# A four-layer megakernel on one core: the prologue and two seams listed in another order, a lead of 80 scores, and the last two token blocks finished one after the other

## The chip, the core and the metric

The kernel runs on one core of a Trainium2 chip. The metric is device time in microseconds (us) for one execution of the whole program. TensorE (PE in the profile, with PEld for its weight loads), VectorE (DVE), ScalarE (ACT), GpSimd (POOL) and SyncE (SP, which issues nearly all DMAs) each run their own queue in order. They wait for each other through semaphores.

## What is computed

The input is `x` of 2 x 2048 x 256 in float32. Four residual layers follow each other, each on a layer norm of `x`:

```python
x = x + attn_a(layernorm(x))     # softmax attention, 16 heads, 4 kv heads, head size 16
x = x + ffn(layernorm(x))
x = x + attn_b(layernorm(x))     # causal linear attention: (q k^T * tril) v, rope, gate, norm
x = x + ffn(layernorm(x))        # the same weights as the first ffn

def ffn(x):
    gf = global_net(x.mean(axis=1))            # 256 -> 128 -> 64 -> 1, gelu, sigmoid
    out = x
    for _ in range(3):
        tf = coupling_net(out)                 # 256 -> 256 -> 128 -> 64 -> 1, gelu, sigmoid
        coupling = 0.1 + adaptive_range * (0.7 * gf + 0.3 * tf - 0.5) * 2
        out = out + coupling * twist(out)      # twist swaps and negates quarters of the features
    return out
```

## The kernel before

The 4096 tokens are eight blocks of 512 (`BLK`), four to each of the two batches. The program is one straight list of instructions. `in_order` (L136 onwards) ties each engine to the order in which the Python code emitted its instructions, so the order of the calls in the source is the order in every queue.

**First attention.** A unit is one block of queries and one of four groups of heads, 32 units in all. `largest()` (L361 to L420) is a generator. Each `next(ahead)` emits one score matmul `s` (L376) into one of three PSUM banks and one VectorE maximum `mx` (L380) over it; there are 64 of them to a unit. After a unit's 64 comes the reduction `nm` (L390) and its split into two parts `mt` (ACT L397, POOL L398). The turn of the maxima `mr` (DVE L403) follows behind the fourth score of the next unit, as `turning.pop()()`, and then eight small DMAs (L407, L412) carry the result to `a_m`. The main loop (from L636) takes a unit in 16 steps `kb`. Each step emits four `next(ahead)`, four score matmuls `p` (L648) with the maximum added by another matmul (L652), four exponentials on ScalarE (L656) and eight passes of `av` (L633) for the step before.

**Prologue.** Before that loop, blocks of `x` arrive and are normalised, turned into feature planes (`features`, L131 and L302), and projected to keys (`keys`, `pk` L309), values (`pv` L326) and queries (`asked`, `pq` L336). `look(j)` (L270 to L276) takes a block's statistics on VectorE and GpSimd. `spread(j)` (L290) normalises it on ScalarE. Keys go through memory and back by DMA (`stored` L246, `fetch` L251). `rows()` is a generator of three pieces. The first issues nine DMAs on SP (L216, eight for the output weights `a_wo`; L217, the bias `a_bo`). The second multiplies the identity by the bias on GpSimd (`a_db`, L221). The third spreads it over the partitions by a matmul (`a_pb`, L226) and copies it out on VectorE (`a_bo_row`, L227); the row is first used by the addition at L467, when the first unit is finished. `pieces()` yields 22 times: six queries of blocks 1 to 3, then for each of the blocks 4 to 7 features, keys, and the two halves of the queries (with the values). The loop over `LEAD` interleaves them with the scores:

```python
LEAD, MORE, WARM = 64 + 10, 6, 6
for n in range(4, LEAD):
    next(ahead)
    if (n % 3 == 1 and n < 55) or (n > 63 and n % 2 == 0):
        next(rest, None)
```

So 17 pieces stand three scores apart, eleven scores then stand alone, and five pieces follow two scores apart. Six scores more (`MORE`) are emitted in odd steps `kb` of unit 0, after which the maxima are 80 ahead.

**The rest.** `behind()` holds the other three layers. `ps` is a ring of seven PSUM banks, and `ps_state` holds one more bank for the running state `b_sums` of the linear attention. In the feed-forward layers, blocks go in pairs `k` (0 to 11: three cycles of four pairs). `first` (L817) and `second` (L827) are the first two matmul layers, `third` (L839) is the third, with both blocks of a pair in one bank and one gelu, and `fourth` is the last layer, the coupling and the addition. In cycles one and two `fourth` works on feature planes with VectorE and GpSimd (L857 to L864). In the last cycle (`back`, L886 onwards) it gives one coupling per token (L891, L896 to L898), turns the planes back (`turn_back`, L875, L879) and adds the twist on VectorE (L912), and in the last layer it stores the block (L918). `context` (L777 onwards) is the global net, a generator: the first `next` reduces the sums on VectorE (`gmf`, L781, L782), the second runs the first matmul (`p1f`, L786).

Two seams are listed by hand. Between the first feed-forward layer and the linear attention, the last pair's `fourth(11)` stands among the queries and keys of block 0 (`zero.query()`, `zero.rotate()`, `zero.key()`). Between the linear attention and the last layer, `x.next_turn()`, `third(1)`, `context` of batch 1, `fourth(1)` and `second(2)` follow each other. The program ends with `second(11)`, in which the two blocks are turned back early (`turn_ahead`), `third(11)` and `fourth(11)`.

Of the kernel before, what the change touches and what calls it, by code (L numbers as in the profile page):

```python
# [11 lines left out]
AF = mybir.ActivationFunctionType  # L12
# [4 lines left out]
P = 128  # L17
# [50 lines left out]
def tile_hybrid(ctx: ExitStack, tc: tile.TileContext, x: bass.AP, consts: bass.AP, wa_d: bass.AP, wf_d: bass.AP, wb_d: bass.AP, out: bass.AP):  # L68
# [28 lines left out]
    def tokens(j):  # L97
        return xs[:, 4 * j : 4 * j + 4, :]
# [54 lines left out]
    def attention_a():  # L153
        with ExitStack() as st:
# [206 lines left out]
            def largest():  # L361


                turning = []
                for u, (j, g) in enumerate(units):
                    k0 = (j // BPB) * N
                    qP = queries[u]
                    mx = sb.tile([P, KV, 4, 4], F32, tag="mx", name=f"mx{u}")
                    first = u == 0

                    def step(kb, qi, r):

# [3 lines left out]
                        mm(  # L376
                            s, qP[r // 2][row, qi * P : (qi + 1) * P],
                            kP[r // 2][row, k0 + kb * BLK : k0 + (kb + 1) * BLK], start=True, stop=True,
                        )
                        nc.vector.tensor_reduce(mx[:, r, qi : qi + 1, kb], s, AX.X, ALU.max)  # L380

                    for kb in range(4):
                        for qi in range(4):
                            for r in (0, 1, 3, 2):
                                step(kb, qi, r)
                                if (kb, qi, r) == (0, 0, 2) and turning:
                                    turning.pop()()
                                yield
                    nm = sb.tile([P, KV, 4], F32, tag="nm", name=f"nm{u}")
                    nc.vector.tensor_reduce(nm, mx, AX.X, ALU.max, negate=True)  # L390

                    mt = sb.tile([P, KV, 2, 4], F32, tag="mt", name=f"mt{u}")
# [24 lines left out]
                    if first or u + 1 == len(units):  # L417
                        turn_maxima()
                    else:
                        turning.append(turn_maxima)  # L420
# [83 lines left out]
                        nc.vector.tensor_tensor(pair, pair, po.rearrange("p (t d) -> p t d", t=2), ALU.add)  # L504
                        yield


            LEAD, MORE, WARM = 64 + 10, 6, 6
            ahead = largest()
            begin = len(nc.cur_bb.bb.instructions)  # L510
            loads = ExitStack()
# [81 lines left out]
            def pieces():  # L593

                memsets()
                look(4)
                values(3)
                for j in range(1, BPB):
                    for m in range(2):
                        asked(j, m)  # L600
                        yield
                        if (j, m) == (2, 0):
                            spread(4, ld, 0)
                next(more)
                for j in range(BPB, NB):
                    features(j, ld, 0)
                    if j + 1 < NB:
                        look(j + 1)
                    yield
                    keys(j, ld)()  # L610
                    if j + 1 < NB:
                        spread(j + 1, ld, 0)
                    yield
                    asked(j, 0)
                    yield
                    asked(j, 1)
# [21 lines left out]
            for u, kb in ((u, kb) for u in range(len(units)) for kb in range(KB)):  # L638
# [85 lines left out]
    def behind(tail):  # L724
# [18 lines left out]
        def bank(name):  # L743
            return ps.tile([P, BLK], F32, tag="ps", name=name)
# [28 lines left out]
        def rotations(n, part, store):  # L773
# [70 lines left out]
            def fourth(k, between=None):  # L844
# [8 lines left out]
                for e in range(2):  # L853
# [9 lines left out]
                    nc.vector.tensor_tensor(z[:, 0, :], z[:, 0, :], t0, ALU.add)  # L863
                    nc.gpsimd.tensor_tensor(z[:, 1, :], z[:, 1, :], t1, ALU.subtract)  # L864

            def turn_back(k, e, h):

                j = blocks(k)[e]
# [9 lines left out]
                for s in range(2):  # L878
                    nc.vector.tensor_tensor(half[:, :, s, :], half[:, :, s, :], tr[:, :, 1 - s, :], ALU.add)  # L879
                return half, tr  # L880

            def turn_ahead(k, e):
                for h in range(2):
# [2 lines left out]
            def back(k, js, a3, between):  # L886
# [12 lines left out]
                for e in range(2):  # L899
                    j = js[e]  # L900
                    if e == 1 and between:
                        between()
                    for h in range(2):
                        half, tr = turned.pop((k, e, h), None) or turn_back(k, e, h)
                        for q in range(2):
                            tile = 2 * h + q

                            x4, t4 = (
                                a.rearrange("p s (u f) -> p (s u) f", u=2) for a in (half[:, q, :, :], tr[:, q, :, :])
                            )  # L910
                            for m, quarters in enumerate((slice(0, 4, 3), slice(1, 3))):
                                nc.vector.scalar_tensor_tensor(  # L912
                                    x4[:, quarters, :], t4[:, quarters, :], cs[:, m, 2 * tile + e : 2 * tile + e + 1],
                                    x4[:, quarters, :], ALU.mult, ALU.add,
                                )
                        if store:
                            s0 = (j % BPB) * BLK + 2 * h * P
                            nc.sync.dma_start(  # L918
                                out[j // BPB, s0 : s0 + 2 * P, :].rearrange("(t p) d -> p t d", p=P),
                                tokens(j)[:, 2 * h : 2 * h + 2, :],  # L920
                            )

            return context, first, second, third, fourth, turn_ahead


        sums1 = hold.tile([P, 2, NB], F32, name="sums1")
# [280 lines left out]

        def rounds(f, n):

            context, first, second, third, fourth, _ = f  # L1210
            k = n // 2
            if n % 2 == 0:
                if 0 <= k - 2:
# [9 lines left out]
                    first(k, 1)  # L1223

        f = rotations(0, sums0, False)
        context, first, second, third, fourth, _ = f
        turned, looked = first_norms, {}

        def block_of(j):
# [92 lines left out]
        one.turn()  # L1322

        f = rotations(1, sums1, True)
        context, first, second, third, fourth, turn_ahead = f
# [211 lines left out]
```

## Time and profile before

| | |
|---|---|
| three timed runs | 2127.65, 2130.35, 2135.94 us; median 2130.35 us |
| the profiled execution | 2133.95 us, of which the span from the first to the last instruction is 2132.2 us |
| mean granted TensorE clock | 0.990 |
| PE busy | 2101.0 us (99%) |
| DVE busy | 1700.7 us (80%) |
| ACT busy | 1427.6 us (67%) |
| POOL busy | 355.6 us (17%) |

The span splits by stage, at the first exponential of unit 0 and the last one of unit 31: the prologue is the first 107.8 us, the softmax attention runs to about 1528 us, the first feed-forward layer to about 1710 us, the linear attention to about 1976 us, and the last layer to the end. Busy time counts matmuls that are waiting inside a pipeline, and their ends are modelled, so 99% doesn't say that TensorE is at its peak. The granted clock is the share of full speed that the hardware let TensorE run at. In a timeline, a row has the start, the length, the engine, the line and operation, the tiles, the count, and in brackets the idle time of that engine before it and what ended it.

### The profile page before, as it was taken

Reading aid. Unit: us, or ns where it says so; the run is one execution under the profiler, and the core shown is the slowest. Engines: PE = TensorE matmul, PEld = TensorE weight load, DVE = VectorE, ACT = ScalarE, POOL = GpSimd, SP = SyncE. Lnnn points to the kernel's source line nnn. Section 1 sums busy time; section 2 is a strip of 40 time slices with the busy share of each in tenths; the row PEclk is TensorE's granted clock in tenths of the full one; section 3 lists DMA queues with packets and bytes.
Section 4 is the critical chain, followed back from the end, with each engine's and each line's share of the span. In section 5 each row is a group of like instructions: output and inputs, shape, how many; then the busy total and the mean of one; then the engine's idle time right before and its main releaser. Section 6 shows DMA issues by size and latency. Waiting matters only on the chain.

```text
span 2132.2 us, 38745 instructions
## 1 busy us (share of the span) xinstructions
PE 2101.0 (99%) x14158; PEld 1018.7 (48%) x14158; DVE 1700.7 (80%) x3241; ACT 1427.6 (67%) x2787; POOL 355.6 (17%) x352
## 2 busy tenths in 40 slices
PE   9899999999999999999999999999999999999998
PEld 4344444444444444444444444444443567776434
DVE  7689998998999999899899899987134688886335
ACT  4377777777777877777777777777864445554443
POOL 3100000001001000000000000000135355551450
PEclk9799999999999999999999999999999999999999
DMA  6320110101101011010110101100100000000002
GB/s 204 92 88 10 49 37 17 47 10 47 37 19 37 18 49 39 18 38 20 47 37 20 37 19 48 38 18 8 52 1 1 0 2 1 2 1 2 0 0 79
DMA packets 59695, 68.71 MB, mean 32 GB/s; under 512 B 24944, under 2 KB 34032, under 8 KB 59248
## 3 DMA queue, kind: packets, MB, share of 16 engines
q1 hardware_dynamic: 58592, 64.79, 11.2%
q8 instruction: 111, 1.82, 0.4%
q10 hardware_dynamic: 720, 0.92, 0.1%
q14 instruction: 80, 0.66, 0.1%
q0 software_dynamic: 192, 0.52, 0.1%
HBM read 35.78 MB, written 26.21 MB: 29 GB/s over the span
## 4 chain that ended last, share of the span: by engine, by line
PE 93%; DVE 3%; issue 1%; ACT 1%; POOL 1%; DMA 1%; SPq 0%; DVEq 0%; POOLq 0%; ACTq 0%
PE av L633 24%; PE s L376 22%; PE p L648 11%; PE q1f L817 8%; PE p L652 7%; PE q2f L827 4%; PE pe L1117 2%; PE bpo L1143 2%; PE po L499 1%; PE pq L975 1%; PE pk L975 1%; PE pw L984 1%; PE pv L984 1%; DVE mx L380 1%; PE q3f L839 1%
## 5 line engine op out<-in xcount | busy, mean ns | idle before, releaser
L380 DVE TENSOR_REDUCE mx<-s 128x1 f32<-128x512 f32 x2048 | 1272.7, 683 | 110.7 <-PE s L376 106.4
L656 ACT ACTIVATE e<-p 128x512 f32<-128x512 f32 x2048 | 1057.7, 603 | 312.8 <-PE p L652 305.9
L376 PE MATMUL s<-a_kP,qP 64*128 64x512 f32 x2048 | 707.0, 471 | 4.8 <-DVE mx L380 2.8
L652 PE MATMUL p<-a_m,a_pick 64*128 64x512 f32 x2048 | 586.5, 415 | 0.0
L376 PEld LDWEIGHTS s<-a_kP,qP 64*128 64x128 f32 x2048 | 283.5, 184 | 567.4 <-DVE mx L380 550.8
L633 PE MATMUL av<-e,a_v 128*32 128x512 f32 x4096 | 546.8, 605 | 0.0
L648 PE MATMUL p<-qP,a_kP 64*128 64x512 f32 x2048 | 527.5, 394 | 2.5 <-ACT e L656 2.5
L648 PEld LDWEIGHTS p<-qP,a_kP 64*128 64x128 f32 x2048 | 286.9, 185 | 64.6 <-ACT e L656 25.5
L652 PEld LDWEIGHTS p<-a_m,a_pick 64*128 64x128 f32 x2048 | 284.6, 184 | 26.1
L817 PE MATMUL q1f<-zq,wf 128*128 128x512 f32 x384 | 175.7, 600 | 0.0
L633 PEld LDWEIGHTS av<-e,a_v 128*32 128x32 f32 x4096 | 81.0, 108 | 129.2 <-issue 121.2
L818 ACT ACTIVATE a1f<-q1f,wf 128x512 f32<-128x512 f32 x96 | 65.8, 686 | 102.2 <-PE q1f L817 99.0
L398 POOL TENSOR_TENSOR mt<-nm,mt 128x16 f32<-128x16 f32 x31 | 6.9, 221 | 736.3 <-ACT mt L397 736.3
L817 PEld LDWEIGHTS q1f<-zq,wf 128*128 128x128 f32 x384 | 70.5, 190 | 97.4 <-issue 84.9
L827 PE MATMUL q2f<-a1f,wf 128*128 128x512 f32 x192 | 90.7, 616 | 0.0
L1123 DVE TENSOR_TENSOR en<-pe,small 128x512 f32<-128x512 f32 x128 | 79.4, 683 | 11.3 <-PE pe L1117 11.2
L237 POOL TENSOR_TENSOR ql<-zq,qh 128x512 f32<-128x512 f32 x15 | 19.3, 1286 | 359.5 <-ACT qh L234 359.5
L858 DVE TENSOR_SCALAR cf<-cf,f_beta,alphaf 128x512 f32<-128x512 f32 x32 | 33.6, 1050 | 54.0 <-ACT cf L857 54.0
L862 POOL TENSOR_TENSOR tf<-cf,zq 128x512 f32<-128x512 f32 x32 | 56.6, 1768 | 93.5 <-DVE cf L858 93.1
L829 ACT ACTIVATE a2f<-q2f,wf 128x512 f32<-128x512 f32 x48 | 32.6, 685 | 53.3 <-PE q2f L827 53.3
L827 PEld LDWEIGHTS q2f<-a1f,wf 128*128 128x128 f32 x192 | 35.6, 195 | 45.8 <-issue 44.7
L864 POOL TENSOR_TENSOR zq<-zq,tf 128x512 f32<-128x512 f32 x32 | 56.8, 1776 | 2.5
(209 smaller groups left out, 1633.5 us busy)
## 6 DMA issues: line engine op xcount, KB each, us to landing
qP<-dq SPq DMA_DIRECT2D x64, 256.0 KB
dq<-qh SPq DMA_DIRECT2D x62, 128.0 KB
dq<-ql SPq DMA_DIRECT2D x62, 128.0 KB
a_kP<-dk SPq DMA_DIRECT2D x16, 256.0 KB
oc<-avs SPq DMA_DIRECT2D x128, 32.0 KB
sums<-dr SPq DMA_DIRECT2D x128, 32.0 KB
out<-xs SPq DMA_DIRECT2D x16, 256.0 KB
xs<-in_x SPq DMA_DIRECT2D x7, 512.0 KB
```

The source lines that it names most:

```text
L376: mm(s, qP[r // 2][row, qi * P : (qi + 1) * P], kP[r // 2][row, k0 + kb * BLK : k0 + (kb + 1) * BLK], start=True, stop=True,)
L380: nc.vector.tensor_reduce(mx[:, r, qi : qi + 1, kb], s, AX.X, ALU.max)
L633: mm(av[32 * r : 32 * r + 32, :], vA[:, units[u][0] // BPB * KB + kb, 32 * r : 32 * r + 32], es[r], start=(kb == 0), stop=(kb == KB - 1),)
L648: mm(t[r], kP[r // 2][row, k0 : k0 + P], qP[r // 2][row, :], start=True, stop=False)
L652: mm(t[r], pick[row, :], mrow[r // 2][row, :], start=False, stop=True)
L656: nc.scalar.activation(es[r], t[r], AF.Exp, scale=1.0 / HD**0.5)
L817: mm(q1, w1[:, c, m * P : (m + 1) * P], z[:, c, :], start=(c == 0), stop=(c == 1))
L818: nc.scalar.activation(a1[:, m, :], q1, AF.Gelu, bias=b1[:, m : m + 1])
L827: mm(q2, w2[:, c, :], a1[:, c, :], start=(c == 0), stop=(c == 1))
L862: nc.gpsimd.tensor_tensor(t1, cs, z[:, 0, :], ALU.mult)
L864: nc.gpsimd.tensor_tensor(z[:, 1, :], z[:, 1, :], t1, ALU.subtract)
L1123: nc.vector.tensor_tensor(self.ens[t][w], pes[w].rearrange("p (h n) -> p h n", h=4), const("triu").unsqueeze(1).to_broadcast([P, 4, P]), A ...
```

## The change

It does six things, all by reordering or splitting work:

1. The six scores of `MORE` leave unit 0. `LEAD` is 80, so ten scores stand in a row at the prologue's end.
2. In the loop over `LEAD`, 19 pieces stand three scores apart (up to score 58), and three come at scores 64, 66 and 69.
3. The second and third pieces of `rows()` (`a_db`, then `a_pb` and `a_bo_row`) both stand in the last piece, behind the values of block 7. The nine DMAs stay where they were.
4. `turn_maxima` stands behind the third score of the next unit and not behind the fourth.
5. At the first hand-listed seam, `fourth(11)` comes directly behind the query of block 0, and rotation and key of block 0 stand between its two blocks. At the second, `third(1)` comes before `x.next_turn()`, and `second(2)` before `fourth(1)`.
6. In the very last pair, each block has its own third layer (64 rows of a bank), its own gelu, its own coupling matmuls (into the bank `b_sums`), tanh and two small VectorE operations. The first block's third layer stands between the second block's `second` and its turn. The first block's additions are emitted before the second block's couplings.

On each engine the instruction lists differ by few entries. PE has four matmuls more, ACT and DVE two operations more each, SP the same DMAs in the same order, and on POOL only `a_db` moves, from before the statistics of block 5 to behind the last keys.

```diff
-                                if (kb, qi, r) == (0, 0, 2) and turning:
+                                if (kb, qi, r) == (0, 0, 3) and turning:
                                     turning.pop()()
...
-            LEAD, MORE, WARM = 64 + 10, 6, 6
+            LEAD, WARM = 64 + 16, 6
...
-                next(more)
                 for j in range(BPB, NB):
                     features(j, ld, 0)
...
                     asked(j, 1)
                     values(j)
-                    if j == BPB:
+                    if j + 1 == NB:
+                        next(more)
                         next(more)
                     yield
...
             for n in range(4, LEAD):
                 next(ahead)
-                if (n % 3 == 1 and n < 55) or (n > 63 and n % 2 == 0):
+                if n % 3 == 1 and n < 61 or n in (64, 66, 69):
                     next(rest, None)
...
-                if kb % 2 == 1 and u * KB + kb < 2 * MORE:
-                    next(ahead)
...
+            def apart(k, e):
+                row = slice(64 * e, 64 * e + 64)
+                q3 = bank(f"q3f{n}_{k}_{e}")
+                mm(q3[row, :], w3, narrow[k][e], start=True, stop=True)
+                a3 = take("en", [P, BLK], f"a3f{n}_{k}_{e}")
+                nc.scalar.activation(a3[row, :], q3[row, :], AF.Gelu, bias=b3[row, :])
+                cs = take("small", [P, 3, 4], f"cf{n}_{k}_{e}")
+                def coupling():
+                    q4 = sums[:, e, 0, 0:4]
+                    for tile in range(4):
+                        mm(
+                            q4[:, tile : tile + 1], a3[row, tile * P : (tile + 1) * P], w4[row, 0:1],
+                            start=True, stop=True, skip_group_check=True,
+                        )
+                    nc.scalar.activation(cs[:, 2, :], q4, AF.Tanh, bias=hb4, scale=0.5)
+                def add():
+                    nc.vector.tensor_scalar(
+                        cs[:, 0, :], cs[:, 2, :], plain, plains[blocks(k)[e] // BPB], ALU.mult, ALU.add
+                    )
+                    nc.vector.tensor_scalar(cs[:, 1, :], cs[:, 0, :], -1.0, None, ALU.mult)
+                    for h in range(2):
+                        half, tr = turned.pop((k, e, h))
+                        twist(half, tr, h, lambda m, tile: cs[:, m, tile : tile + 1])
+                        keep(blocks(k)[e], h)
+                return coupling, add
...
         third(11)
         zero.query()
+        def amid():
+            zero.rotate()
+            zero.key()
+        fourth(11, amid)
         zero.rotate()
-        zero.key()
-        fourth(11, zero.rotate)
         zero.narrow()
...
         first(2, 1)
+        third(1)
         x.next_turn()
-        third(1)
         next(front1)
+        second(2)
         fourth(1)
         next(front1)
-        second(2)
         first(3, 0)
...
-        second(11, lambda e: turn_ahead(11, e))
-        third(11)
-        fourth(11)
+        last = []
+        def behind_second(e):
+            if e == 1:
+                last.append(apart(11, 0))
+            turn_ahead(11, e)
+        second(11, behind_second)
+        last[0][0]()
+        last.append(apart(11, 1))
+        last[0][1]()
+        last[1][0]()
+        last[1][1]()
```

`twist` and `keep` are the four VectorE additions and the store of half a block, taken out of `back` unchanged.

More of the change, by code (lines that the diff above doesn't have):

```diff
@@ L864, in fourth, with twist, keep @@
                     nc.gpsimd.tensor_tensor(z[:, 1, :], z[:, 1, :], t1, ALU.subtract)
+            def twist(half, tr, h, coupling):
+                for q in range(2):
+                    x4, t4 = (a.rearrange("p s (u f) -> p (s u) f", u=2) for a in (half[:, q, :, :], tr[:, q, :, :]))
+                    for m, quarters in enumerate((slice(0, 4, 3), slice(1, 3))):
+                        nc.vector.scalar_tensor_tensor(
+                            x4[:, quarters, :], t4[:, quarters, :], coupling(m, 2 * h + q), x4[:, quarters, :],
+                            ALU.mult, ALU.add,
+                        )
+            def keep(j, h):
+                s0 = (j % BPB) * BLK + 2 * h * P
+                nc.sync.dma_start(
+                    out[j // BPB, s0 : s0 + 2 * P, :].rearrange("(t p) d -> p t d", p=P),
+                    tokens(j)[:, 2 * h : 2 * h + 2, :],
+                )
             def turn_back(k, e, h):
@@ L880, in turn_back @@
                 return half, tr
+            def apart(k, e):
[11 more added lines that the diff above has]
+                            start=True, stop=True, skip_group_check=True,
+                        )
+                    nc.scalar.activation(cs[:, 2, :], q4, AF.Tanh, bias=hb4, scale=0.5)
+                def add():
+                    nc.vector.tensor_scalar(
+                        cs[:, 0, :], cs[:, 2, :], plain, plains[blocks(k)[e] // BPB], ALU.mult, ALU.add
+                    )
+                    nc.vector.tensor_scalar(cs[:, 1, :], cs[:, 0, :], -1.0, None, ALU.mult)
[4 more added lines that the diff above has]
+                return coupling, add
             def turn_ahead(k, e):
@@ L904, in back @@
                         half, tr = turned.pop((k, e, h), None) or turn_back(k, e, h)
[L905 to L915, printed above, removed]
-                        if store:
[L917 to L923, printed above, removed]
+                        twist(half, tr, h, lambda m, tile: cs[:, m, 2 * tile + e : 2 * tile + e + 1])
+                        if store:
+                            keep(j, h)
+            return context, first, second, third, fourth, turn_ahead, apart
         sums1 = hold.tile([P, 2, NB], F32, name="sums1")
@@ L1208, in rounds @@
         def rounds(f, n):
-            context, first, second, third, fourth, _ = f
+            context, first, second, third, fourth, *_ = f
             k = n // 2
@@ L1225, in behind @@
         f = rotations(0, sums0, False)
-        context, first, second, third, fourth, _ = f
+        context, first, second, third, fourth, *_ = f
         turned, looked = first_norms, {}
@@ L1324, in behind @@
         f = rotations(1, sums1, True)
-        context, first, second, third, fourth, turn_ahead = f
+        context, first, second, third, fourth, turn_ahead, apart = f
         front, front1 = context(0), context(1)
```

## The prediction, made before the changed kernel ran

> **What bounds the kernel now.** I read the chain of waits first, then PE's idle times by window, then timelines of the places where it idles. The chain says that TensorE's own work ends nearly everything:
>
> ```profile
> PE 93%; DVE 3%; issue 1%; ACT 1%; POOL 1%; DMA 1%; SPq 0%; DVEq 0%; POOLq 0%; ACTq 0%
> ```
>
> So time is to be had only where PE stands still or is clocked down: 2132.2 - 2101.0 = 31.2 us idle, and the spells at half clock. The list of waits of the prologue (total us, times, longest) names the largest stop:
>
> ```profile
> ACT z L290 <- POOL nb_a L276: 13.8, 3, 11.8
> POOL a_db L221 <- DMA a_bo<-in_wa: 23.1, 1, 23.1
> PE a_pb L226 <- POOL a_db L221: 5.4, 1, 5.4
> ```
>
> GpSimd sat at `a_db` for 23.1 us until the bias landed. Behind it in POOL's queue stood block 5's statistics, and so ScalarE's `z` waited 11.8 us; PE stood at `a_pb`. PE's timeline has the stop, and later a run of eleven scores at VectorE's pace:
>
> ```profile
> 54.61 0.46 PE L326 MATMUL pv<-small,kv 64*128 64x64 f32 x4
> 60.43 1.22 PE L226 MATMUL a_pb<-a_db,small 128*128 128x256 f32 x2 [5.37 <-POOL a_db L221]
> 64.36 0.47 PE L131 MATMUL tr<-small,z 128*128 128x128 f32 x1 [1.40 <-ACT zq L342]
> ...
> 83.36 1.10 PE L376 MATMUL s<-a_kP,qP 64*128 64x512 f32 x5
> 84.93 1.70 PE L376 MATMUL s<-a_kP,qP 64*128 64x512 f32 x4 [0.47 <-DVE mx L380]
> 87.92 1.39 PE L376 MATMUL s<-a_kP,qP 64*128 64x512 f32 x3 [1.29 <-DVE mx L380]
> 89.23 3.78 PE L336 MATMUL pq<-zb,a_wq 128*128 128x512 f32 x4
> ```
>
> The same `pq` takes 1.98 us elsewhere: the clock had dropped. Windows (length, busy time by engine, granted clock) show what each idle stretch sets off:
>
> ```profile
> 53.60:57.04 3.44, 1.46 (x7) 0.51 (x5) 1.16 (x2) 0.00 (x0) 0.00 (x0) 1.00 0.86 273
> 57.04:70.69 13.65, 8.86 (x20) 4.31 (x20) 6.03 (x17) 4.64 (x9) 4.34 (x7) 0.50 0.34 85
> 70.69:87.76 17.07, 15.14 (x53) 6.44 (x52) 15.21 (x33) 8.63 (x16) 3.73 (x4) 1.00 0.40 94
> 87.76:101.41 13.65, 13.49 (x28) 6.04 (x28) 7.03 (x15) 2.18 (x5) 0.00 (x0) 0.50 0.13 40
> 1992.40:1999.22 6.82, 6.12 (x10) 3.04 (x11) 4.58 (x6) 1.02 (x3) 5.83 (x4) 0.50 0.00 0
> ```
>
> Each spell follows a stretch of some 3.4 us in which PE was mostly idle, and lasts 6.8 to 13.65 us. Units 0 and 1, cut at their first exponentials, with the maxima counted:
>
> ```profile
> 107.76:156.51 48.75, 43.96 (x72) 1.00 0.31 93
> 156.51:199.78 43.27, 39.76 (x65) 1.00 0.05 12
> ```
>
> Unit 0 is 5.48 us longer and holds seven maxima more. The second seam, with its stop and its slow `q2f`:
>
> ```profile
> 1990.00 1.13 PE L852 MATMUL q4f<-a3f,wf 64*128 64x512 f32 x4 [0.79 <-ACT a3f L841]
> 1993.10 1.01 PE L786 MATMUL p1f<-gmf,wf 128*128 128x1 f32 x4 [1.97 <-DVE gmf L782]
> 1993.98 6.28 PE L827 MATMUL q2f<-a1f,wf 128*128 128x512 f32 x8
> ```
>
> And the end, where VectorE waits for the last coupling:
>
> ```profile
> 2124.43 0.29 DVE L897 TENSOR_SCALAR cf<-cf,f_plain,plainf 128x8 f32<-128x8 f32 x1 [1.16 <-ACT cf L896]
> 2124.83 4.22 DVE L912 SCALAR_TENSOR_TENSOR xs<-trf,cf,xs 128x128 f32<-128x128 f32 x16
> ```
>
> **The change part by part.**
>
> *(a) Prologue up to the first `p`.* `a_db` and `a_pb` leave the place of the stop. SP's nine DMAs stay (53.2 to 58.3 us), so block 4's keys are still stored late, but these serve batch 1, due in unit 16. Block 6 needs block 4's key buffers again only some 10 us after that store. Each block's round is then as block 4's was, at full clock: from its turn at 45.44 to the end of `pv` at 55.07, plus three scores, 0.73: 10.3 us. Block 5's turn comes at 55.8, block 6's at 66.1, block 7's at 76.4. Block 7's data was issued at 51.73 and memory traffic falls off by 60. From 76.4 VectorE paces: 24 maxima at 0.605 (14 took 8.45) = 14.5; the key cast 0.42; `nm` to `mr` of unit 0, 0.88 (90.89 to 91.77); the bias row's copy 0.42; and about 1.5 in which VectorE waits for `a_pb`, which stands behind a `pq` of 1.98. First `p` at 76.4 + 17.7 = 94.1, before at 106.99: **-12.9**. Bounds: rounds of 11.5 when a `look` stops PE each time (block 4 lost 0.4 so), -10; no wait at `a_pb`, -14.4. `a_m` isn't late: the chain from `mr` to landing was 6 us (91.6 to about 97.6) and starts near 83.
>
> *(b) Unit 0 without the six scores.* It becomes like unit 1: 5.48 at most, 6 x 0.605 = 3.6 at least. Two of its steps take 3.53 for work that may stay. **-5.0**.
>
> *(c) The clock.* Ten scores in a row at VectorE's pace (6 us) are like the run of 83.4 to 89.2, so I expect a half-clock spell again, now falling on unit 0. In unit 1 a step takes 2.70, of which VectorE waits 0.22 and PE's chain is about 2.48, or 4.96 at half clock: (4.96 - 2.70)/4.96 = 0.456 lost per us. Of 13.65 us, some 3 fall in the run and cost nothing: 10.65 x 0.456 = **+4.9**. Bounds: 0 (no spell) and 6.2 (all of it).
>
> The Trainium skill, TensorE: Matmul & The Clock Gate, Part 1, "What's actually happening", says that the full clock comes back after at least one busy window of about 3.4 us. The 13.65 us spell from 87.76, with PE 13.49 us busy, speaks against so quick a return. By the page about 3.4 us of spell would fall on the loop, an estimate of 1.6 us, and the forecast would be 2108.
>
> *(d) `mr` one score earlier.* **0**, 31 times. It took the 0.22 us in which VectorE waited for the next step's score. Now it stands before the group's last maximum: 2.48 + 0.2 still fits into 2.70, and `mt` is ready (GpSimd ends it at 189.0, the third maximum ends at 190.3). If that cover is gone: 31 x 0.2 = 6.2.
>
> *(e) First seam.* PE's idle time of 1709 to 1720 is 0.49 + 1.47 + 0.51 + 0.21 + 0.65 = 3.3. The 1.47 (a bank held by block 0's additions) goes, since keys now take banks between the two blocks. But `pt` needs the rotated key, whose shuffles now stand behind four additions' worth of VectorE work (3.75), while the second block's 3.75 moves ahead of the key's last addition. By the rows that addition lands within 1 us of where it did. **0**, from -3.3 to +2.2 (two additions at 1.74 beside GpSimd and not 0.64).
>
> *(f) Second seam.* PE's list from 1987.2, with the lengths of the rows before: `q3f` 1.08, turn 1.04, `q2f` 3.60 (its length at full clock), `q4f` 1.13, `p1f` 0.5: `first(3,0)` at 1994.5, not at 2000.09: **-5.6**. `gmf` still ends at 1993.05, in front of `p1f` at 1994.0. What waits behind it, `gh1f` on ScalarE, is next needed one `first` later. The coupling of pair 1 comes 3 us later on GpSimd and is due in pair 5, some 15 us on. If the clock drops all the same, 6.28 - 3.60 of it is lost: -2.9.
>
> *(g) End.* PE: `q3f` of block 0 ends at 2120.9, the turn at 2121.9, `q4f` 1.05 (as many passes per block as both had together) ends at 2123.0, tanh at 2123.3. VectorE, done with its turns at 2123.27, starts at 2123.35: two small operations 0.46, eight additions 2.11. Block 1: `q3f`, gelu 0.69, `q4f` 1.05, tanh at 2125.7, before VectorE is free at 2125.9; then 0.46 + 2.11: 2128.5, before 2129.05. **-0.55**, from 0 to -1.16 (the whole wait). The last store follows alike.
>
> **Sum**: -12.9 - 5.0 + 4.9 + 0 + 0 - 5.6 - 0.55 = -19.15. From the profiled 2133.95 (span 2132.2 and 1.75 around it) that gives 2114.8. That execution lies 3.6 above the median of the runs, 2130.35, from which the sum gives **2111**.
>
> **Rivals.**
>
> *VectorE takes the prologue over.* It was busy 15.21 of 17.07 us from 70.69. Rounds of 11.5 cost 2.4 more, and if unit 0's 3.05 us steps come from VectorE lagging behind after the run, not from the six scores, the 5.0 stays: 2118.6. Against it: steps 13 to 15 of unit 0, right after the last extra score, already take 2.70.
>
> *No spell in unit 0.* The drops fall on a grid of 3.41 us. With a kind position, or if the scores at 64 to 69 keep PE busy enough, (c) is nothing: 2106. Against it: 6 us of sparse work hold at least most of one window.
>
> *The second seam doesn't gain its clock.* The third layer or `gmf` makes PE wait again: 2111 + 2.7 = 2114.
>
> *Slower: half clock holds through unit 0.* One mechanism, in unit 0. After the run, PE's work in a step (2.48 of 2.70 when clocked fully) is cut into pieces between VectorE's releases, and the clock never gets its busy window. 16 steps x 2.26 = 36 in place of 4.9: 2142. It decides from (19.15 + 4.9)/0.456 = 53 us of half clock on. For it: the clock stayed down for 13.65 us though PE was 99% busy. Against it: no spell of this run is longer, and at half clock PE is the bound and has no gaps.
>
> **How the numbers follow.** Forecast 0.56 (its own range 2107 to 2116), VectorE 0.16, no spell 0.14, seam 0.05, slower 0.05, and 0.04 for what I didn't see. Range: 2102 (no spell, (a) at -14.4, (b) at -5.5, (e) at -1.5) to 2121 (VectorE, with (d) at some 2.5). No change means within 0.5%, 2119.7 to 2141.0, about what this kernel's runs can tell. Of VectorE's 0.16 some 0.05 lies there, of the unseen 0.03: faster 0.87, same 0.08, slower 0.05.
>
> **What would show it.** Right: no idle PE at `a_pb`, `z` of block 5 near 52; first `p` near 94; unit 0 near 43.8 plus the clock's share, a 0.50 window in or before it; units 1 to 3 still 43.27; no 0.50 window near 1990; at the end no wait above 0.2 before the last pair's couplings. Wrong: units longer than 43.3 (d), `pt` of block 0 more than 18 us behind its first `pq` (before: 1698.93 to 1716.82), or a first `p` after 98.

## The result, and the profile after

The changed kernel takes 2110.09 us (median of 4 runs, 2109.47 to 2110.38), the kernel before beside it 2132.62 (4 runs, 2127.65 to 2135.94): a ratio of 0.9896, with a 95% interval from 0.9874 to 0.9918. Between the two profiled executions the span fell from 2132.2 to 2108.4, by 23.8 us. TensorE (PE) is now idle for 18.4 us in place of 31.2. The table cuts both executions at the same events and puts the prediction's terms beside the differences.

| stretch (us) | before | after | difference | predicted |
|---|---|---|---|---|
| start to the first `p` | 106.99 | 93.54 | -13.45 | (a) -12.9 |
| first `p` to first exponential | 0.77 | 1.29 | +0.52 | in (c) |
| unit 0 | 48.75 | 43.28 | -5.47 | (b) -5.0, (c) +4.9 |
| units 1 to 31 | 1371.64 | 1372.41 | +0.77 | (d) 0 |
| first seam: block 0's first `pq` to first `pe` | 20.91 | 20.29 | -0.62 | (e) 0 |
| second seam: `first(2,1)` to `first(3,0)` | 16.46 | 10.62 | -5.84 | (f) -5.6 |
| end: last second half of a `q1f` to the end | 18.03 | 18.21 | +0.18 | (g) -0.55 |

The chain that ended last, by engine, in the changed kernel:

```profile
PE 96%; DVE 2%; DMA 1%; ACT 1%; issue 0%; POOL 0%; SPq 0%; DVEq 0%; ACTq 0%; POOLq 0%
```

PE's share rose from 93 to 96%: time in which PE waited went. Half clock time is not told apart in this share; PE's busy time fell too, from 2101.0 to 2090.0. PE's timeline of the prologue (start, length, instruction; in brackets the idle time before it and who ended it):

```profile
56.31 1.09 PE L131 MATMUL tr<-small,z 128*128 128x128 f32 x8
...
66.40 1.09 PE L131 MATMUL tr<-small,z 128*128 128x128 f32 x8
...
76.41 1.09 PE L131 MATMUL tr<-small,z 128*128 128x128 f32 x8
...
86.85 0.70 PE L226 MATMUL a_pb<-a_db,small 128*128 128x256 f32 x2
87.48 0.73 PE L376 MATMUL s<-a_kP,qP 64*128 64x512 f32 x3
88.76 5.57 PE L376 MATMUL s<-a_kP,qP 64*128 64x512 f32 x9 [0.54 <-DVE mx L380]
93.54 1.21 PE L647 MATMUL p<-qP,a_kP 64*128 64x512 f32 x2
```

The turns of blocks 5, 6 and 7 stand 10.1 and 10.0 us apart, and no idle time is left in front of `a_pb`. Nine scores then take 5.57 us, at VectorE's pace, and the first `p`'s go at half speed. The windows say why (length, busy time of PE, PEld, DVE, ACT and POOL with their counts, granted clock, DMA share, GB/s):

```profile
86.30:90.07 3.77, 3.02 (x13) 1.40 (x12) 2.48 (x5) 0.95 (x2) 0.00 (x0) 1.00 0.66 141
90.07:96.90 6.83, 6.83 (x20) 3.84 (x22) 6.46 (x12) 1.88 (x4) 0.00 (x0) 0.50 0.73 245
94.83:138.11 43.28, 43.28 (x317) 19.93 (x315) 39.70 (x66) 33.86 (x67) 3.84 (x3) 0.98 0.27 81
138.11:181.41 43.30, 43.30 (x324) 19.24 (x320) 40.19 (x68) 33.73 (x67) 0.22 (x1) 1.00 0.05 13
```

The half clock spell that the prediction expected is there, but it is 6.83 us long and began 3.47 before the first `p`, so only 3.36 of it fell on the loop. The second seam, on PE's timeline:

```profile
1970.97 3.60 PE L824 MATMUL q2f<-a1f,wf 128*128 128x512 f32 x8
1974.49 1.13 PE L849 MATMUL q4f<-a3f,wf 64*128 64x512 f32 x4
1975.55 0.61 PE L783 MATMUL p1f<-gmf,wf 128*128 128x1 f32 x4
1976.02 3.68 PE L814 MATMUL q1f<-zq,wf 128*128 128x512 f32 x8
```

PE waits for nothing, and `q2f` takes 3.60 and not 6.28. At the end VectorE still waits, now twice:

```profile
2099.69 0.29 DVE L915 TENSOR_SCALAR cf<-cf,f_plain,plainf 128x4 f32<-128x4 f32 x1 [0.30 <-ACT cf L912]
...
2102.57 0.29 DVE L915 TENSOR_SCALAR cf<-cf,f_plain,plainf 128x4 f32<-128x4 f32 x1 [0.33 <-ACT cf L912]
...
2102.98 2.15 DVE L868 SCALAR_TENSOR_TENSOR xs<-trf,cf,xs 128x128 f32<-128x128 f32 x8
```

### The profile page after: what moved, and what is told of

It reads as the page before. It is cut to its first block, busy times and chain, and to the rows that moved or that the text cites. A ratio compares the mean times of both kernels' runs of the same rounds, so it can differ in the third digit from the quotient of the medians.

```text
span 2108.4 us, 38765 instructions
## 1 busy us (share of the span) xinstructions
PE 2090.0 (99%) x14166; PEld 1011.6 (48%) x14166; DVE 1697.3 (81%) x3243; ACT 1428.4 (68%) x2789; POOL 355.2 (17%) x352
## 3 DMA queue, kind: packets, MB, share of 16 engines
q1 hardware_dynamic: 58592, 64.79, 11.3%
## 4 chain that ended last, share of the span: by engine, by line
PE 96%; DVE 2%; DMA 1%; ACT 1%; issue 0%; POOL 0%; SPq 0%; DVEq 0%; ACTq 0%; POOLq 0%
PE av L632 24%; PE s L376 23%; PE p L647 12%; PE q1f L814 8%; PE p L651 7%; PE q2f L824 4%; PE pe L1147 2%; PE bpo L1173 2%; PE po L499 1%; PE pq L1005 1%; PE pw L1014 1%; PE pv L1014 1%; PE pk L1005 1%; PE q3f L836 1%; PE pq L336 1%; DVE mx L380 1%
## 5 line engine op out<-in xcount | busy, mean ns | idle before, releaser
L491 POOL TENSOR_TENSOR oc<-oc,sums 128x512 f32<-128x512 f32 x16 | 20.6, 1284 | 210.2 <-DMA sums<-dr 150.5
```

## The experiments

Twelve runs were made in three groups of four, each group on one chip, with the kernel before beside it. Two of the twelve are the changed kernel itself once more. Medians are compared within a group.

| kernel | median (us) | runs from .. to | first `p` | unit 0 |
|---|---|---|---|---|
| group 1: before | 2130.52 | 2126.78 .. 2136.65 | | |
| the changed kernel again | 2108.87 | 2107.82 .. 2109.62 | 93.60 | 43.10 |
| old end | 2108.42 | 2106.47 .. 2109.50 | 93.68 | 43.46 |
| `mr` behind the fourth score | 2108.93 | 2108.74 .. 2109.43 | 93.62 | 43.26 |
| `mr` and another end | 2108.77 | 2108.42 .. 2109.32 | 93.49 | 44.08 |
| group 2: before | 2132.26 | 2128.64 .. 2136.39 | | |
| old second seam | 2115.61 | 2114.10 .. 2118.18 | 93.71 | 43.94 |
| old first seam | 2111.52 | 2110.35 .. 2112.05 | 93.83 | 43.89 |
| bias pieces early | 2121.85 | 2120.99 .. 2122.85 | 105.17 | 44.07 |
| lead of 74, six inside | 2111.73 | 2111.12 .. 2111.99 | 90.56 | 48.66 |
| group 3: before | 2129.70 | 2126.42 .. 2132.88 | | |
| the changed kernel, third time | 2108.45 | 2106.59 .. 2110.11 | 93.38 | 44.42 |
| spread pieces | 2108.98 | 2107.73 .. 2110.50 | 94.52 | 42.78 |
| spread pieces, old end | 2108.45 | 2105.84 .. 2109.69 | 93.69 | 42.98 |
| before, bias pieces late | 2116.21 | 2115.82 .. 2116.97 | 93.87 | 48.77 |

### The bias pieces put back, and moved alone

In the changed kernel, put back:

```diff
+                next(more)
                 for j in range(BPB, NB):
...
-                    if j + 1 == NB:
-                        next(more)
+                    if j == BPB:
                         next(more)
```

> Only the two pieces of the prologue that load and multiply the bias row go back to the places they had: before block 4's round and at its end. Theory: GpSimd sits at a_db some 23 us again, block 5's statistics and z are late by some 12 us, PE stands at a_pb for about 5, the clock drops for one spell more, and together this gives back most of the 13.45 us by which the first p came earlier: first p 104 to 107, 10 to 13 slower. Rival: the bias stop is worth the 5.4 us of PE idle time alone, and the other 8 came from the pieces being spread otherwise: first p near 99, 5 to 6 slower.

In the kernel before, the reverse of this diff and nothing else:

> The kernel before with one edit: the two pieces with the bias row move behind the last block's values. Theory, the reverse of putting them back: the first p comes 10 to 13 us earlier than 106.99, and the kernel is 9 to 12 faster than before. Rival: the bias stop is worth its 5.4 us alone, and the rest needs the pieces' new spacing.

Put back, they cost 11.3 to 11.6 us of the first `p` (105.17; the two kernels of its group with the pieces late have 93.71 and 93.83, the changed kernel 93.54). PE's timeline of that kernel has the old stop again, now 5.92 long, and the stretch around it falls to half clock:

```profile
55.71 0.46 PE L326 MATMUL pv<-small,kv 64*128 64x64 f32 x4
62.09 1.22 PE L226 MATMUL a_pb<-a_db,small 128*128 128x256 f32 x2 [5.92 <-POOL a_db L221]
```

```profile
58.98:72.63 13.65, 9.15 (x20) 4.32 (x20) 6.03 (x17) 4.65 (x9) 4.34 (x7) 0.50 0.33 85
```

Moved alone in the kernel before, they bring the first `p` from 106.99 to 93.87, by 13.12, and the median from 2129.70 to 2116.21. This is more than the 9 to 12 expected; the rival, the 5.4 us of idle PE alone, falls in both kernels. So one late load was worth over twice the idle time that it showed: the rest stands behind the stop, where ScalarE, in the kernel with the pieces put back, waits 12.4 us for block 5's statistics before it can start `z`, and PE runs at half clock. The turns in the two profiles of the second pair say how the 13.12 add up. Block 5's turn comes at 56.65 and not 64.36 (7.7), block 6's at 66.74 and not 76.99 (2.5 more, a round that ran at half clock), and the last 2.9 come after that, where a later spell was 6.83 long and not 13.65. That these 2.9 belong to the bias stop is not shown, as the pieces put back cost 11.3 to 11.6 only.

### The lead put back to 74

```diff
-            LEAD, WARM = 64 + 16, 6
+            LEAD, MORE, WARM = 64 + 10, 6, 6
...
+                if kb % 2 == 1 and u * KB + kb < 2 * MORE:
+                    next(ahead)
```

> Only the lead goes back: 74 scores ahead and six more inside unit 0. Theory: the prologue's last run at VectorE's pace is shorter by 6 x 0.605 = 3.6, unit 0 longer by 5.4, so 1.8 slower than the changed kernel, and more by up to 3 if a half clock spell falls on the loop: 2 to 5 slower. Rival: six scores cost the same on either side, no difference within 0.5.

Neither is met. The first `p` (90.56) comes 3.2 to 3.3 earlier than in its two neighbours with the bias pieces late, unit 0 is 48.66, and unit 1 starts at 140.38, 1.4 behind the 139.00 of the kernel with the old first seam. The median is 2111.73; the neighbour's 2111.52 less the 0.6 that its seam costs is 2110.9, so the lead of 80 gains 0.8 by medians and 1.4 by the profiles, and the expected 2 to 5 were too much. The 2110.9 is worked out; the changed kernel itself did not run on this chip. The windows of unit 0, VectorE's maxima alone (DVE busy and count, clock, DMA share, GB/s), first of this kernel, then of the kernel before with its bias pieces late, which also has six scores inside:

```profile
91.72:140.38 48.66, 43.36 (x70) 0.97 0.31 94
```

```profile
94.55:143.32 48.77, 43.95 (x72) 1.00 0.29 91
```

Here the 3.41 us of half clock that followed the first `p` (91.18 to 94.59) cost little: from the first `p` to unit 1 it is 49.82 us with them and 49.45 without, with 71 and 72 maxima in between. That is 0.4 us, or 1.0 if the missing maximum is counted at 0.6; at the price worked out below, 0.42 for each us, it would be 1.4. With six scores more VectorE paces much of unit 0, and a slow PE is partly covered.

With these kernels the way from 106.99 to 93.54 can be split, in one order of the edits:

| kernel | bias pieces | other pieces | lead | first `p` |
|---|---|---|---|---|
| before | early | old | 74 | 106.99 |
| before, bias pieces late | late | old | 74 | 93.87 |
| changed, lead of 74 | late | new | 74 | 90.56 |
| changed | late | new | 80 | 93.54 |
| changed, bias pieces early | early | new | 80 | 105.17 |

Bias -13.1, spacing -3.3, lead +3.0. In the other order the bias comes last: spacing and lead together -1.8 (106.99 to 105.17), bias -11.6. What the spacing removes is seen in the second row's kernel, on PE's timeline:

```profile
73.10 3.33 PE L376 MATMUL s<-a_kP,qP 64*128 64x512 f32 x9
77.69 1.39 PE L376 MATMUL s<-a_kP,qP 64*128 64x512 f32 x3 [1.25 <-DVE mx L380]
79.01 3.78 PE L336 MATMUL pq<-zb,a_wq 128*128 128x512 f32 x4
```

A run of twelve scores without a piece between them (by these rows; the prediction counted eleven), PE waiting for VectorE, a clock that drops at 76.21, and a `pq` of 3.78 where 1.98 is usual.

### The second seam put back

```diff
         first(2, 1)
-        third(1)
         x.next_turn()
+        third(1)
         next(front1)
-        second(2)
         fourth(1)
         next(front1)
+        second(2)
```

> Only the second seam's order goes back (third(1) behind next_turn, second(2) behind fourth(1)). Theory, the prediction's step (f): 5.8 slower than the changed kernel, first(2,1) to first(3,0) 16.5 and not 10.6, with idle PE of 0.8 and 2.0 us and a half clock spell of 6.8 us behind it that doubles the q2f. Rival: the seam is worth its idle time alone, 2 to 3 us, and no spell comes back because the windows of 3.41 us lie otherwise.

PE's timeline of that kernel:

```profile
1971.99 1.13 PE L849 MATMUL q4f<-a3f,wf 64*128 64x512 f32 x4 [0.79 <-ACT a3f L838]
1975.10 0.61 PE L783 MATMUL p1f<-gmf,wf 128*128 128x1 f32 x4 [1.98 <-DVE gmf L779]
1975.57 5.38 PE L824 MATMUL q2f<-a1f,wf 128*128 128x512 f32 x8
1980.78 3.60 PE L814 MATMUL q1f<-zq,wf 128*128 128x512 f32 x8
```

The seam is 15.16 and not 10.62: 4.54 more, made of the two waits (2.77) and of 1.78 in `q2f` (5.38 to 3.60). The spell came back, so the rival falls, but 3.41 us long and not 6.83; the median is 2115.61, 4.7 above the 2110.9 worked out above for the changed kernel on this chip, with single runs up to 2118.18. The seam is worth 4.5 to 5.8, by how the spell falls.

### The first seam put back

```diff
-        def amid():
-            zero.rotate()
-            zero.key()
-
-        fourth(11, amid)
         zero.rotate()
+        zero.key()
+        fourth(11, zero.rotate)
```

> Only the first seam's order goes back (rotate and key before fourth(11), the second rotate in the middle of it). Theory: 0.6 slower than the changed kernel; from block 0's first pq to the first pe 20.9 and not 20.3, with the 1.47 us wait of pv for a bank back and the 1.42 us wait of pt gone. Rival, the prediction's step (e): no difference.

PE's waits between 1680 and 1705 (total, times, longest), first of that kernel, then of the changed one:

```profile
PE pv L1014 <- DVE xs L868: 1.5, 1, 1.5
PE pt L1026 <- DVE rotk L1073: 0.7, 2, 0.5
```

```profile
PE pt L1026 <- DVE rotk L1073: 1.7, 2, 1.4
```

The old order waits 2.2 us at these two places, the new one 1.7, and the stretch is 20.93 against 20.29: the new order gains 0.64. The theory holds, and the other profiles agree: the stretch is 20.91 to 20.93 in all three executions with the old order, and 20.25 to 20.29 in nine of eleven with the new one (20.74 and 21.10 in the two others, into which a spell at half clock fell). Some 1.0 of the 1.5 that `pv` no longer waits is given back at `pt`, whose key is rotated later.

### The place of `mr`

```diff
-                                if (kb, qi, r) == (0, 0, 3) and turning:
+                                if (kb, qi, r) == (0, 0, 2) and turning:
```

The edit, and the changed kernel as it is beside it:

> Only the chain from mr to the bias row goes back behind the fourth score of a unit's first group. Theory: the later place costs the 0.77 us that units 1 to 31 gained in sum (43.30 and not 43.27 each), so this kernel is 0.8 faster than the changed one and its units 1 to 3 are 43.27. Rival, the prediction's step (d): no difference, and units of 43.30 that stem from the prologue's other order.

> The changed kernel as it is, as the scale for its neighbours. Median 2110.1, its runs within 1 us of each other. In the profile: unit 0 within 0.1 of unit 1 (43.28), and no more than 4 us of half clock behind the first p.

The theory falls. This kernel's units 1 to 3 are 43.29, 43.29 and 43.25, and its median is 2108.93 against 2108.87. The changed kernel itself, run again, had units of 43.22, 43.20 and 43.20 with `mr` at its new place. The 0.77 us of the table belong to the execution and not to the kernel; step (d)'s nothing was right. What was expected of the second execution itself was met in part: its spell reached 2.78 us behind the first `p`, within the 4, but unit 0 was 0.12 below its unit 1, the median 1.2 below 2110.1, and its runs spread over 1.8 us.

### The end put back, and another end

```diff
-        second(11, behind_second)
-        last[0][0]()
-        last.append(apart(11, 1))
-        last[0][1]()
-        last[1][0]()
-        last[1][1]()
+        second(11, lambda e: turn_ahead(11, e))
+        third(11)
+        fourth(11)
```

> Only the end goes back: both blocks of the last pair take layers 3 and 4 together again, as in the kernel before. My theory after the result: splitting was worth nothing, because layer 3 of one block alone takes as long on PE (1.07) as both blocks' together (1.08 to 1.11): this kernel 0.2 faster than the changed one, from the last q1f to the end 18.0 and not 18.2. Rival, the prediction's step (g): 0.55 slower than the changed one.

The old end takes 18.03 from the same mark, the new one 18.20 on the same chip; medians 2108.42 and 2108.87, with overlapping runs. The theory's 0.2 is what the profiles show: 18.02 or 18.03 in all four with the old end, 18.20 or 18.21 in eight of nine with the new one. They speak against a loss of 0.55 by the old end. The ninth, the changed kernel's third execution, took 18.81: its clock fell 11.3 us behind the mark, in the eight others 12.0 to 14.4. With the old end it fell at 10.1 to 11.4 and cost nothing, as its couplings are done on PE 9.9 us behind the mark and those of the new end's second block at 12.1. PE's timelines, of the kernel before and of the changed kernel:

```profile
2121.14 1.11 PE L839 MATMUL q3f<-a2f,wf 128*64 128x512 f32 x4
```

```profile
2096.28 1.07 PE L900 MATMUL q3f<-a2f,wf 128*64 128x512 f32 x2
...
2099.29 1.07 PE L900 MATMUL q3f<-a2f,wf 128*64 128x512 f32 x2
```

Four passes of both blocks take 1.11, two passes of one block take 1.07. In the records the passes of the two blocks start in pairs, 0.01 to 0.04 us apart, each with its own half of the array's columns. The Trainium skill, TensorE: Matmul & The Clock Gate, Part 3, "The mechanism", says that matmuls on separate tiles of the array overlap; these rows agree. Taken apart, the blocks lose that, and PE has about 1.0 more to do in all (2 x 1.07 - 1.11), in front of block 1's coupling.

The other end takes block 0's third layer ahead of block 1's second, and has `mr` at its old place:

```diff
         def behind_second(e):
-            if e == 1:
-                last.append(apart(11, 0))
             turn_ahead(11, e)
+            if e == 0:
+                last.append(apart(11, 0))
```

> The changed kernel with mr behind the fourth score and with layer 3 of block 0 of the last pair issued before block 1's second layer, so that its coupling is ready when VectorE ends the first turn. Theory: 0.8 from mr, and about 0.5 at the end, where VectorE no longer waits 0.30 for block 0's coupling and 0.33 for block 1's: 1.3 faster than the changed kernel, from the last q1f to the end 17.7. Rival: PE's chain of block 1 sets the end whatever the order before it, and only the 0.8 comes.

18.11 for the end and 2108.77 in all. VectorE still waits 0.30 and 0.27 us for the two couplings, so the rival's reading of the end holds, and there was nothing to come from `mr`.

### The last pieces of the prologue spread

```diff
                     asked(j, 1)
-                    values(j)
                     if j + 1 == NB:
                         next(more)
+                        yield
+                    values(j)
+                    if j + 1 == NB:
+                        yield
                         next(more)
...
-                if n % 3 == 1 and n < 61 or n in (64, 66, 69):
+                if n % 3 == 1 and n < 61 or n in (64, 68, 72, 75, 78):
```

> The changed kernel once more, on the chip of its three neighbours: 2108.9 to 2111, unit 0 of 41.9 + 0.42 for each us of the half clock spell behind the first p, and other units anywhere from 43.20 to 43.33, all alike.

> The changed kernel with the last pieces of its prologue spread over the last run of scores: behind scores 64, 68, 72, 75 and 78 in place of 64, 66 and 69, with pv and the bias row each in a piece of its own. Nothing is added or left out. Theory: VectorE paces this run, so its wait of 1.53 us for a_pb goes and the first p comes about 1.5 earlier, near 92.1; and as PE's work is spread out, the clock drops later or not at all, which takes up to 1.4 from unit 0: 1.5 to 2.9 faster than the control. Rival: the pieces now make VectorE wait for scores elsewhere and a drop comes all the same, only later and so wholly on unit 0 (6.83 x 0.42 = 2.9): within 0.5 of the control or up to 1.5 slower.

> The same spread pieces, and the end of the kernel before (both blocks of the last pair take layers 3 and 4 together). Theory: 0.17 faster than the run with the spread pieces alone, which 5 rounds may not tell from nothing; from the last q1f to the end 18.03 and not 18.20. Rival, the prediction's step (g): 0.55 slower.

The first `p` came at 94.52, and with the same spread pieces and the old end at 93.69, against 93.38: later, and not 1.5 earlier. Counted from block 7's turn, ahead of which the edit changes nothing, it is 17.92 and 17.65 against 17.13, so 0.5 to 0.8 later. VectorE's waits from 76.5 to the first `p` (total, times, longest), with the pieces spread, and in the changed kernel:

```profile
DVE mx L380 <- PE s L376: 3.1, 4, 1.1
```

```profile
DVE a_bo_row L227 <- PE a_pb L226: 1.5, 1, 1.5
DVE mx L380 <- PE s L376: 0.6, 1, 0.6
```

The wait of 1.5 is gone, but now each `pq` of 1.98 makes VectorE wait 1.13 for the next score. In unit 0 (42.78 and 42.98) the two kernels gained, as less of their spell fell on it. The rival is right: the medians, 2108.98, 2108.45 and with the old end 2108.45, can't be told apart. The control met its expectation in unit 0 (44.42, where 41.9 + 0.42 x 5.95 is 44.4), and its median lies 0.45 below the 2108.9 given. No version here beats the changed kernel by more than its runs differ.

### What the half clock costs unit 0

Eleven of the profiles have the lead of 80 and a spell that reaches into unit 0, of different lengths. Some of them, with the time between the first `p` and the spell's end:

| kernel | spell at half clock | behind the first `p` | unit 0 |
|---|---|---|---|
| spread pieces | 92.66 to 96.07 | 1.55 | 42.78 |
| changed, again | 92.97 to 96.38 | 2.78 | 43.10 |
| changed | 90.07 to 96.90 | 3.36 | 43.28 |
| `mr` and another end | 91.77 to 98.60 | 5.11 | 44.08 |
| changed, third time | 92.50 to 99.33 | 5.95 | 44.42 |

A line through all eleven is 42.06 + 0.39 for each us, and none lies more than 0.12 from it. The spells are counted from the first `p`, and unit 0 starts 1.1 to 1.3 us later. With the time from the first `p` to unit 1 in place of unit 0 the line is 43.23 + 0.42, and none lies more than 0.15 from it. So a us at half clock costs 0.39 to 0.42 here (the prediction worked out 0.456). No kernel ran without a spell, so 43.23 is the line's value and not a measured one.

Ahead of the first `p`, where VectorE sets the pace, half clock cost nothing. From block 7's turn to the first `p` it is 17.11 to 17.13 us in all eight profiles that have the changed prologue's pieces and lead, whether 0.6 or 3.6 us of half clock lay in that stretch. The spell with the longest share in the loop; PE is shown as busy through it, at half speed:

```profile
92.50:99.33 6.83, 6.76 (x29) 4.14 (x32) 6.09 (x11) 3.81 (x8) 0.00 (x0) 0.50 0.81 311
```

## Why the prediction was right, and where it wasn't

The forecast was 2111 in 2102 to 2121, faster; measured 2110.09. The causes of the gain were the ones it named, and the two large ones are shown by edits: the bias pieces moved in both directions, the second seam put back. Its sum of -19.15 was short, though, of the -23.8 of the profiled executions and of the -22.5, -21.65 and -21.25 between medians. Nearly the whole gap is unit 0: (b) and (c) add up to -0.1, and from the first `p` to unit 1 the table has -4.95. That 2111 was met so closely is partly luck: the sum was too small, but it was taken from 2130.35, and the kernel before stood at 2132.62 beside the changed kernel.

(a) Right, cause and size: -12.9 predicted, -13.45 measured; rounds of 10.3 predicted, 10.0 to 10.1 measured; block 7's turn at 76.4 predicted, 76.41 measured, and from there 17.7 predicted, 17.13 measured; 1.5 at `a_pb`, 1.53 measured. That the bias row's pieces carry it is shown by moving them alone (-13.1, and 11.3 to 11.6 put back). The new spacing and the longer lead nearly cancel (-3.3 and +3.0).

(b) Right in kind, too small. From the first `p` to unit 1 the kernel before took 49.52; by the line's 43.23, unit 0 without its six scores and without a spell is 6.3 shorter, not 5.0. The prediction kept a part back for two steps of 3.53 "for work that may stay"; it seems not to have stayed. Unit 0 is even shorter than unit 1 where least of a spell fell on it (42.78 and 42.98 against 43.20). This fits with its first step, which has no `av` of a step before it (8 passes, 1.06 us); this is argued.

(c) This term was mis-sized: "Of 13.65 us, some 3 fall in the run and cost nothing: 10.65 x 0.456 = +4.9." The spell came where it was forecast, and its price of 0.456 was near the 0.39 measured. Its length was wrong. It took the longest spell of the trace for the rule. In the twelve profiles of kernels with the new spacing, the spells that reach into the loop last 3.41 or 6.83 and end within 6 us of the first `p`; in the changed kernel that is 3.36 x 0.42 = 1.4 us and not 4.9. The page of the Trainium skill that the prediction weighed (TensorE: Matmul & The Clock Gate, Part 1, "What's actually happening": full clock after at least one busy window) was nearer than the row, with the estimate of 1.6 worked out from it. The three spells of 13.65, two in the kernel before and one behind the bias stop put back, stand behind or in sparse PE work; why the one from 87.76 lasted so long with PE shown as busy stays open. One reading needs a limit: in the kernel before, the three spells that the prediction lists follow 3.41 us in which PE was busy for only 1.4 to 1.6. In the changed kernel PE was shown as busy for 2.67 of the 3.41 us ahead of the drop at 90.07, and in the kernel before with its bias pieces late for 3.16 of those ahead of 76.21. So a mostly idle stretch is not needed; which share of busy time is enough is not shown.

(d) Right, but only the second execution of the same kernel showed it; from one pair of profiles alone the wrong cause, the place of `mr`, looked like 0.77 us. The sign of being wrong, units longer than 43.3, came up too (43.31, and 43.33 elsewhere), so it was no sign of this step.

(e) 0 predicted, -0.62 and -0.64 measured. The exchange was as described, `pv`'s wait against `pt`'s, and the remainder was called zero. `pt` came 17.2 behind block 0's first `pq`, inside the 18 given as a sign.

(f) Right, cause and size: -5.6 predicted, -5.84 measured, 4.5 put back, by the spell's length.

(g) Wrong in sign. By "`q3f` of block 0 ends at 2120.9" one block's third layer gets at most 0.7 us of PE (from 2120.18, where the turn had stood); it takes 1.07. The step that failed is that splitting the third layer costs PE next to nothing; it costs 1.0 in all, because the blocks' passes used to run side by side. So the tanh of block 0 came 0.34 and that of block 1 0.83 later, from the same mark, than the prediction's times. The sign named, no wait above 0.2, failed too: 0.30 and 0.33, which make up most of the 0.73 between -0.55 and +0.18.

The rivals: VectorE did not take the prologue over, the seam did gain its clock, and no half clock held through unit 0. "No spell" was wrong about the spell and nearly right about its cost.

## What to carry to other kernels

Price a late load by everything queued behind the instruction that waits for it, and by the half clock that follows, not by the idle time at the stop: 5.4 us of idle PE were worth 11 to 13. A slow clock cost nothing here ahead of the first `p`, where VectorE set the pace, and 0.4 per us in unit 0, where PE did, so weigh a spell by how much of it falls on PE-paced work. Two matmuls that use half of the array's columns each may be running side by side; splitting them by time cost 1.0 us of PE here.

## What the runs showed of the hardware

- The loop's pace differs between executions of one kernel. Units 1 to 31 of the changed kernel took 1372.41 in one execution and 1370.25 in another, the first of these units 43.30 or 43.31 in the one and 43.20 to 43.22 in the other, while the stretch from the last exponential to the first `pq` was 170.78 in both. That is 2.2 us, nearly all of the 2.3 between these two executions (2110.14 and 2107.82). In the second group all four kernels had 43.31 to 43.33. The cause stays open.
- Whether a spell comes at all varies as well: the changed kernel had one of 3.41 us at 315 in two executions, and in the third one in the first seam, at 1696.76, which lengthened that seam from 20.29 to 20.74.
- The 28 runs of the kernel before spread over 10 us (2126.42 to 2136.65); with its bias pieces late the four runs lay within 1.2 (2115.82 to 2116.97). The granted clock goes along with the time: in the 24 runs of the three groups it is 0.989 to 0.991 in all above 2132.5 and 0.992 to 0.994 in all below 2130. So it is time at half clock that varies. The bias stop alone doesn't bring this: put back into the changed kernel, it left five runs within 1.9 us (2120.99 to 2122.85). What in the kernel before does stays open.
